# A second tile transposed by TensorE, and loads moved between three DMA queues, in a conditional-mix and paged-attention kernel

## The chip, the cores and the metric

The kernel runs on one core of one Trainium2 chip. A core has five engines that run side by side and wait for one another through semaphores: TensorE (PE; its weight loads are listed as PEld), VectorE (DVE), ScalarE (ACT), GpSimd (POOL) and SyncE (SP), which here only issues DMAs. The metric is the device time of one execution in microseconds (us); the median of several runs counts. The profile is one further execution, with every instruction and every DMA packet recorded.

## The reference

The input `x` has 64 sequences of 32 tokens with 512 channels, in float32. Two layers are added to it in turn:

```python
# layer 0: a matrix chosen per sequence mixes its 32 rows
x = x + einsum('bct,bcd->bdt', x, weights[condition])
# layer 1: attention over a paged cache
q = rope(rmsnorm(x @ Wq.T))            # 32 heads of 128
k = rope(rmsnorm(x @ Wk.T)); v = x @ Wv.T   # 8 heads of 128
kc, vc = k_cache[block_table], v_cache[block_table]   # 16 pages of 32 keys per sequence
scores = q . [kc, k] / sqrt(128)       # 4 query heads share a key head
scores = where(valid, scores, -1e30)   # cached keys: position < cache_seqlens
x = x + (softmax(scores) @ [vc, v]) @ Wo.T
```

The sequence lengths run from 207 to 1644 and the cache holds 512 keys for each sequence, so many sequences have some masked keys. Where the sums of the exponentials leave a safe range, the kernel runs a second, exact pass; with these inputs it is not entered, and its code is only counted by a test at the end.

## The kernel before, in words

Four sequences (32 rows each) make a tile of 128 rows, so there are 16 tiles (`NT`). The eight key heads are done in two halves (`NHH`) of four (`GH`), each with its four query heads (`REP`). A `Step` is one tile in one half: steps 0 to 15 are the first half, steps 16 to 31 the second. In the second half a step doesn't mix and transpose its input again: it reads the transposed tile `x1t` and the running sum `acc` back from DRAM, where the first half stored them (`x1t_d`, line 371, and `acc_d`, line 532).

For a step the work is as follows.

- `x1_a`, `x1_c`, `x1_b` (lines 344 to 371): load `x`, mix it (`pmix`), transpose it (`px1t`) into `x1t`. In the second half `x1_t` (line 350) loads `x1t` instead. `x1t` has one buffer.
- `k_a`, `q_a(g)`, `v_a` (lines 493 to 507): eight matmuls each of 128 x 512 (four chunks, each in two passes), into one of four PSUM buffers called `pp`; then `norm_rope` (line 409): a square on ACT, a power on POOL, and six operations on VectorE.
- The normalized queries and keys must be transposed into columns, `q_cols` for the first three sequences of the tile and `q_last` for the fourth. `q_cols` has one buffer, `q_last` two. There are two ways. For step 0 (`by_tensor`, line 473), `to_columns` (line 483) transposes a group with four TensorE instructions into PSUM (`pt`) and copies it out with two ACT copies. For all later steps `turn_rows` (line 451) transposes 32 x 32 blocks on VectorE, and `spread` (line 463) puts the blocks in place with 16 DMAs of SP, four for each sequence.
- For each sequence (`Batch`, line 540): 16 K pages are loaded by SP (`load_k`, line 280; two buffers); VectorE copies one head at a time into key order (`head_keys`, line 560); `scores` and `values` are matmuls, with the exponential on ACT between them. The V rows are gathered by POOL with indirect DMAs, 128 rows at a time into one of three buffers called `raw` (`fetch`, line 311), and ACT multiplies them by the mask on the way to their place (`fill`, line 552). `new_scores` and `new_values` do the same for the tile's own 32 keys.
- `out_proj` (line 512): 32 matmuls of 128 x 512 and an add into `acc`.

The order is written out by hand. SP and PE take their instructions in program order throughout; the other engines do so in the opening (up to `opening.close()`, line 864), and afterwards a planner orders them. The opening holds step 0's projections and the first sequences, and also the second step's keys and values (`k_a(second)`, `v_a(second)`, lines 849 to 851).

The loop at line 909 takes a step in 16 slots, four for each sequence (`bt`), one head (`g`) per slot. In each slot stand the scores of this head, one piece of the *next* step from the table `pieces` (line 866), and the values of the head before. So the next step's keys and queries are projected in slots 3 to 7, spread in slots 9 and 11, and its values projected in slot 13. Half of the previous step's output projection stands in slot 8 and half in slot 9. At the start of each `bt` the K pages of the sequence two ahead are issued (`after = Batch(...)`, line 917), so in slot 12 the sixteen pages come before the `x1_t` of slot 13 (line 956) in SP's queue. Step 0 enters the loop at slot 4 and has no output projection in slots 8 and 9.

Weights: `load_w` (line 234) loads a matrix of 1 MB. An output matrix is loaded in parts, each part two DMAs of 256 KB (line 249). In the opening SP loads the query weights of groups 0, 2 and 3 and the values' weights, POOL the keys' weights and query group 1 (lines 765 to 785). The output weights of the second half are loaded by POOL's queue in steps 16 and 17 (`second_outputs`, line 908); they take the place of the first half's, which are used last in slot 9 of step 16, and are themselves used first in slots 8 and 9 of step 17. The page numbers and lengths, from which the rows to gather and the masks are made, are loaded by POOL (`pages_at`, `lens_at`, lines 793 to 796) and used by VectorE in `cached_rows` (line 160).

## Time and profile before

| | us |
|---|---|
| median of 3 runs | 2183.66 (2181.93 to 2184.26) |
| the profiled execution's own time | 2188.01 |
| its span, first to last instruction | 2186.2 |
| granted TensorE clock, mean | 0.995 |
| share of the chain that ended last: PE | 95% |
| the same: DMA / issue / DVE | 2% / 1% / 1% |
| mean of one matmul of 128 x 512 in `pp_q` | 0.594 |
| mean of one transpose `pt` (128 x 128) | 0.272 |
| mean of one VectorE transpose of `rows` | 0.706 |
| mean of one ACT copy of `pt`, 384 / 128 columns | 0.480 / 0.289 |
| DMA moved | 358.78 MB, mean 164 GB/s |

In the page each row names a line of the kernel, an engine, an operation and the tiles as out<-in. "Idle before" is the time for which the engine stood still ahead of that row's instructions, followed by what ended most of it. In a list of waits the columns are the total in us, the number of times, and the longest. In a timeline a row has its start and its length in us, and in brackets the idle time ahead of it. Matmuls overlap in the pipeline, so a group of eight that "takes" 1.06 us lets the next one start after 0.89. A wait for several semaphores is put down to the one that was signalled last, which need not be the one that mattered.

### The profile page before, as it was taken

Reading aid. Unit: us, or ns where it says so; the run is one execution under the profiler, and the core shown is the slowest. Engines: PE = TensorE matmul, PEld = TensorE weight load, DVE = VectorE, ACT = ScalarE, POOL = GpSimd, SP = SyncE. Lnnn points to the kernel's source line nnn. Section 1 sums busy time; section 2 is a strip of 40 time slices with the busy share of each in tenths; the row PEclk is TensorE's granted clock in tenths of the full one; section 3 lists DMA queues with packets and bytes.
Section 4 is the critical chain, followed back from the end, with each engine's and each line's share of the span. In section 5 each row is a group of like instructions: output and inputs, shape, how many; then the busy total and the mean of one; then the engine's idle time right before and its main releaser. Section 6 shows DMA issues by size and latency. Waiting matters only on the chain.

```text
span 2186.2 us, 41553 instructions
## 1 busy us (share of the span) xinstructions
PE 2150.5 (98%) x12970; PEld 1498.3 (69%) x12970; DVE 1199.1 (55%) x2881; ACT 866.9 (40%) x1574; POOL 813.1 (37%) x1024
## 2 busy tenths in 40 slices
PE   8889999999999999999999999999999999999998
PEld 5657776677766677766776667777667777667775
DVE  5655556665465554555554556545556445556442
ACT  3434444444333444333433334443334433334441
POOL 4433333343333433343334434333334333334330
PEclk9999999999999999999999999999999999999999
DMA  8665555556555555556767655555555555555651
GB/s 245 172 166 161 169 159 150 153 159 171 157 152 142 167 161 165 158 146 195 237 176 198 174 154 165 167 163 163 149 158 162 170 163 160 149 160 158 175 159 57
DMA packets 386839, 358.78 MB, mean 164 GB/s; under 512 B 54736, under 2 KB 316896, under 8 KB 386608
## 3 DMA queue, kind: packets, MB, share of 16 engines
q1 hardware_dynamic: 340608, 210.90, 34.3%
q0 software_dynamic: 42992, 140.86, 22.6%
q10 hardware_dynamic: 3008, 4.25, 0.5%
q8 instruction: 106, 1.74, 0.3%
q14 instruction: 125, 1.02, 0.2%
HBM read 302.59 MB, written 12.58 MB: 144 GB/s over the span
## 4 chain that ended last, share of the span: by engine, by line
PE 95%; DMA 2%; issue 1%; DVE 1%; ACT 0%; SPq 0%; POOL 0%; ACTq 0%; DVEq 0%; POOLq 0%
PE po_x L631 21%; PE ps_x L573 20%; PE pout_x L519 20%; PE pp_q_x L404 19%; PE pp_k_x L404 5%; PE pp_v_x L404 5%; PE pnv_x L615 2%; PE psn_x L591 1%; DMA raw_x<-in_vc_dram,v_row 1%; PE pmix_x L360 1%; DMA pages_at<-in_pages_v_dram 0%; DMA x1t_x<-x1t_d 0%; DMA k_t_x<-in_kt_dram 0%; PE px1t_x L368 0%; SPq L468 0%
## 5 line engine op out<-in xcount | busy, mean ns | idle before, releaser
L318 POOL DMA_INDIRECT raw_x<-in_vc_dram,v_row x512 | 538.2, 1051 | 828.3 <-ACT v_x L331 756.2
L581 ACT ACTIVATE pr_x<-ps_x 128x512 f32<-128x512 f32 x512 | 305.7, 597 | 818.2 <-PE ps_x L573 757.3
L631 PEld LDWEIGHTS po_x<-v_x,pr_x 128*128 128x128 f32 x4096 | 516.1, 192 | 129.8 <-issue 115.4
L631 PE MATMUL po_x<-v_x,pr_x 128*128 128x129 f32 x4096 | 551.6, 278 | 4.9 <-ACT v_x L331 1.9
L404 PE MATMUL pp_q_x<-wq_x,x1t_x 128*128 128x512 f32 x1024 | 462.5, 594 | 3.4 <-ACT kh_x L564 3.4
L519 PE MATMUL pout_x<-wo_x,ot_x 128*128 128x512 f32 x1024 | 450.2, 592 | 0.0
L573 PE MATMUL ps_x<-q_cols_x,kh_x 128*128 128x128 f32 x3072 | 405.7, 275 | 0.5 <-ACT q_cols_x L488 0.2
L573 PEld LDWEIGHTS ps_x<-q_cols_x,kh_x 128*128 128x128 f32 x3072 | 376.3, 192 | 17.1 <-issue 16.6
L331 ACT ACTIVATE v_x<-raw_x,valid 128x512 f32<-128x512 f32 x512 | 363.2, 716 | 16.5 <-DMA raw_x<-in_vc_dram,v_row 16.5
L519 PEld LDWEIGHTS pout_x<-wo_x,ot_x 128*128 128x128 f32 x1024 | 189.7, 190 | 214.3 <-issue 214.3
L404 PEld LDWEIGHTS pp_q_x<-wq_x,x1t_x 128*128 128x128 f32 x1024 | 185.4, 191 | 188.8 <-issue 185.2
L566 DVE COPY kh_x<-k_t_x 128x512 f32<-128x512 f32 x506 | 206.1, 417 | 191.8 <-PE ps_x L573 162.0
L649 DVE TENSOR_TENSOR nv_x<-po_x,nv_x 128x258 f32<-128x258 f32 x256 | 108.3, 423 | 317.7 <-PE po_x L631 282.5
L421 POOL TENSOR_TENSOR rs_q_x<-ms_q_x,minus_half 128x4 f32<-128x4 f32 x128 | 140.2, 1096 | 175.9 <-DVE ms_q_x L419 174.8
L414 ACT ACTIVATE sq_q_x<-pp_q_x 128x512 f32<-128x512 f32 x128 | 76.4, 597 | 271.9 <-PE pp_q_x L404 165.3
L573 PE MATMUL ps_x<-q_last_x,kh_x 128*128 128x128 f32 x1024 | 135.2, 275 | 2.9 <-DVE kh_x L566 2.9
L527 DVE TENSOR_TENSOR acc_x<-pout_x,acc_x 128x512 f32<-128x512 f32 x32 | 22.1, 692 | 199.5 <-PE pout_x L519 199.5
L573 PEld LDWEIGHTS ps_x<-q_last_x,kh_x 128*128 128x128 f32 x1024 | 124.6, 192 | 3.1 <-issue 3.1
L404 PE MATMUL pp_k_x<-wk_x,x1t_x 128*128 128x512 f32 x256 | 118.1, 605 | 2.8 <-DMA x1t_x<-x1t_d 2.5
L418 DVE TENSOR_REDUCE ms_q_x<-sq_q_x 128x4 f32<-128x512 f32 x128 | 86.4, 675 | 53.2 <-ACT sq_q_x L414 51.2
L404 PE MATMUL pp_v_x<-wv_x,x1t_x 128*128 128x512 f32 x256 | 115.2, 592 | 0.0
L652 DVE TENSOR_TENSOR o_x<-nv_x,rden 128x256 f32<-128x256 f32 x256 | 108.5, 424 | 6.5
(106 smaller groups left out, 1472.3 us busy)
## 6 DMA issues: line engine op xcount, KB each, us to landing
k_t_x<-in_kt_dram SPq DMA_DIRECT2D x2048, 64.0 KB
q_cols_x<-rows_x SPq DMA_DIRECT2D x372, 80.0 KB
q_last_x<-rows_x SPq DMA_DIRECT2D x124, 80.0 KB
raw_x<-in_vc_dram,v_row POOLq DMA_INDIRECT x512
acc_x<-in_x_dram SPq DMA_DIRECT2D x16, 256.0 KB
x1t_d<-x1t_x ACTq DMA_DIRECT2D x16, 256.0 KB
wo_x<-in_wo_dram SPq DMA_DIRECT2D x16, 256.0 KB
acc_d<-acc_x SPq DMA_DIRECT2D x16, 256.0 KB
```

The lines of the kernel that those rows point to most:

```text
L318: nc.gpsimd.indirect_dma_start(out=raw.rearrange("p g d -> p (g d)"), out_offset=None, in_=vc, in_offset=bass.IndirectOffsetOnAxis(ap=v_ro ...
L331: nc.scalar.activation(v_bufs[b % 2][:, c, :, 0:D], raw, AF.Copy, scale=ok)
L404: nc.tensor.matmul(pp, st.x1t[:, c, :], w[:, c, :], start=(c == 0), stop=(c == KC - 1))
L418: nc.vector.tensor_reduce(ms, sq, AX.X, ALU.add)
L421: nc.gpsimd.tensor_tensor(rs, ms, minus_half, ALU.pow)
L519: nc.tensor.matmul(st.po, st.ot[:, i, :], wt["o", st.hh, i // 4][:, i % 4, :], start=(i == 0), stop=(i == QH - 1),)
L566: last["dve"] = nc.vector.tensor_copy(k, ba.k_raw[:, :, g, :]).ins
L573: nc.tensor.matmul(ps[:, c, :], ba.k[g][:, c * P : (c + 1) * P], queries(ba, g), start=True, stop=True,)
L581: last["act"] = nc.scalar.activation(pr, ps, AF.Exp, scale=SCALE).ins
L631: nc.tensor.matmul(ba.po[:, g % 2, :], ba.pr[g][:, c, :], ba.v_t[:, c, g, :], start=(c == 0), stop=(c == VC - 1),)
L649: nc.vector.tensor_tensor(t, ba.po, t, ALU.add)
L652: nc.vector.tensor_tensor(ba.o[:, both, :], t[:, :, 0:D], rd.unsqueeze(2).to_broadcast([P, 2, D]), ALU.mult,)
```

## The change

Four edits are made together.

1. The second step's keys and queries are transposed as the first step's are: `by_tensor` holds for `st.n < 2`. `pieces(second)` has no `spread`; instead `to_columns` stands in slots 12 (keys, group 0), 13 (group 1) and 14 (groups 2 and 3). The keys are copied out of PSUM by ACT, the four query groups by VectorE. `v_a(second)` moves from the opening to slot 13.
2. In the opening the query weights of group 2 are loaded on POOL's queue, ahead of `pages_at`, instead of SP's.
3. When the sequence two ahead is loaded at the start of slot 12 (`bt == BT - 1`), only its first eight K pages are issued there; the other eight follow in slot 13, behind `x1_t`.
4. The second half's output weights are issued by SP instead of POOL, at other slots: one part in slot 10 of step 16 and seven parts in slots 2 to 7 of step 17.

```diff
--- before.py
+++ after.py
@@ -246,15 +246,15 @@
             if kind == "o" and not exact:
                 src = src.rearrange("(h j p) e -> h p j e", h=REP, p=S)
                 for h in range(part.start, part.stop):
-                    eng.dma_start(t[h * S : (h + 1) * S, :, :], src[h])
+                    nc.sync.dma_start(t[h * S : (h + 1) * S, :, :], src[h])
                 return
             eng.dma_start(t[:, part, :], src.rearrange("(c p) e -> p c e", p=P)[:, part, :])
 
-        def load_parts(which, hh, at, eng=nc.sync):
+        def load_parts(which, hh, at):
 
             if 0 <= at < 2 * len(which):
                 kind, g = which[at // 2]
-                load_w(kind, hh, g, slice(at % 2 * 2, at % 2 * 2 + 2), eng)
+                load_w(kind, hh, g, slice(at % 2 * 2, at % 2 * 2 + 2))
 
         outputs = [("o", g) for g in range(GH)]
 
@@ -277,7 +277,7 @@
 
         last_k = []
 
-        def load_k(hh, b):
+        def load_k(hh, b, first_pages):
             k_raw = kv.tile([P, NPP, GH, PSIZE], F32, tag="k_t", name=f"k_t_{hh}_{b}_{uid}")
 
             with ExitStack() as order:
@@ -290,7 +290,7 @@
                     max_val=PAGES - 1,
                     skip_runtime_bounds_check_because="a block table names pages of the cache",
                 )
-            for j in range(NPP):
+            def load_page(j):
                 ins = nc.sync.dma_start(
                     k_raw[:, j, :, :].rearrange("p g r -> p (g r)"),
                     kt[hh, bass.ds(page[j], 1)].rearrange("o d e -> (o d) e"),
@@ -303,8 +303,11 @@
                             bass.ds(page[j], 1), hh
                         ].rearrange("o r g d -> (o r) g d"),
                     )
-            last_k[:] = [ins.ins]
-            return k_raw
+                last_k[:] = [ins.ins]
+
+            for j in range(first_pages):
+                load_page(j)
+            return k_raw, [lambda j=j: load_page(j) for j in range(first_pages, NPP)]
 
         raws = {}
 
@@ -471,7 +474,7 @@
                     )
 
         def by_tensor(st):
-            return st.n == 0 or exact
+            return st.n < 2 or exact
 
         def finish(st, i, pp, name, kind):
 
@@ -480,15 +483,13 @@
             else:
                 turn_rows(st, i, norm_rope(st, pp, name, kind), name)
 
-        def to_columns(st, i):
+        def to_columns(st, i, copy=nc.scalar.copy):
 
             pt = transposed(rows[:, :, i, :], f"{i}_{st.name}")
             p4 = pt.rearrange("p h (b s) -> p b h s", b=BT)
             n = BT - 1
-            nc.scalar.copy(q_cols[:, :, i, :].rearrange("p b (h s) -> p b h s", h=4), p4[:, 0:n])
-            nc.scalar.copy(
-                columns(st, n)[:, i, :].rearrange("p (h s) -> p h s", h=4), p4[:, n]
-            )
+            copy(q_cols[:, :, i, :].rearrange("p b (h s) -> p b h s", h=4), p4[:, 0:n])
+            copy(columns(st, n)[:, i, :].rearrange("p (h s) -> p h s", h=4), p4[:, n])
 
         def k_a(st):
             name = f"k_{st.name}"
@@ -540,12 +541,12 @@
         class Batch:
 
 
-            def __init__(self, st, bt):
+            def __init__(self, st, bt, first_pages=NPP):
                 self.st, self.bt = st, bt
                 self.n = st.n * BT + bt
                 self.name = f"{st.name}_{bt}"
                 self.b = st.t * BT + bt
-                self.k_raw = load_k(st.hh, self.b)
+                self.k_raw, self.pages_left = load_k(st.hh, self.b, first_pages)
                 self.k, self.pr = {}, {}
                 self.v_t = v_bufs[self.b % 2]
 
@@ -777,8 +778,8 @@
         nc.scalar.dma_start(cond_row, cond.rearrange("(i s) t -> s t i", s=S)[0:1])
         load_w("k", 0, eng=nc.gpsimd)
         load_w("q", 0, 1, eng=nc.gpsimd)
+        load_w("q", 0, 2, eng=nc.gpsimd)
         batch = Batch(first, 0)
-        load_w("q", 0, 2)
         load_w("v", 0)
         x1_a(second)
         load_w("q", 0, 3)
@@ -848,7 +849,6 @@
         rot_tables(second)
         k_a(second)
         q_b(first, 3)
-        v_a(second)
         scores(batch, 3)
         new_scores(first)
         scores(later, 0)
@@ -864,7 +864,21 @@
         opening.close()
 
         def pieces(st):
-            do = {
+            if st is second:
+                by_vector = nc.vector.tensor_copy
+                return {
+                    4: (lambda st: q_a(st, 0),),
+                    5: (lambda st: q_a(st, 1),),
+                    6: (lambda st: q_a(st, 2),),
+                    7: (lambda st: q_a(st, 3),),
+                    12: (lambda st: to_columns(st, GH), lambda st: to_columns(st, 0, by_vector)),
+                    13: (v_a, lambda st: to_columns(st, 1, by_vector)),
+                    14: (
+                        lambda st: to_columns(st, 2, by_vector),
+                        lambda st: to_columns(st, 3, by_vector),
+                    ),
+                }
+            return {
                 2: (rot_tables,),
                 3: (k_a,),
                 4: ((q_a, 0),),
@@ -875,9 +889,6 @@
                 11: ((spread, (2,)),),
                 13: (v_a,),
             }
-            if st is second:
-                do[2] = do[3] = do[13] = ()
-            return do
 
         def count(hh):
 
@@ -905,7 +916,14 @@
         load_cond_weights(2)
         for at in (3, 4, 5):
             load_parts(outputs, 0, at)
-        second_outputs = [(0, 10), (0, 13), (0, 15), (1, 1), (1, 3), (1, 4), (1, 5), (1, 6)]
+        second_outputs = {
+            (0, 10): (0,),
+            (1, 2): (1,),
+            (1, 4): (2,),
+            (1, 5): (3, 4),
+            (1, 6): (5, 6),
+            (1, 7): (7,),
+        }
         for st in steps:
             ahead = steps[st.n + 1] if st.n + 1 < len(steps) else None
             beyond = steps[st.n + 2] if st.n + 2 < len(steps) else None
@@ -914,7 +932,7 @@
                 this, after = batch, None
                 n = st.n * BT + bt + 2
                 if n < NHH * NT * BT:
-                    after = Batch(steps[n // BT], n % BT)
+                    after = Batch(steps[n // BT], n % BT, NPP // 2 if bt == BT - 1 else NPP)
                     unfilled += [(after, c) for c in range(VC)]
                 for g in range(GH):
                     slot = bt * GH + g
@@ -952,8 +970,11 @@
                             load_cond_weights(beyond.t)
                         if slot == 11:
                             x1_a(beyond)
-                    if slot == 13 and beyond:
-                        x1_t(beyond)
+                    if slot == 13:
+                        if beyond:
+                            x1_t(beyond)
+                        for load in after.pages_left if after else ():
+                            load()
                     if slot == 14 and beyond:
                         x1_c(beyond)
                     if slot == 15 and beyond:
@@ -962,9 +983,8 @@
                         count(0)
                     if st.n == 1 and slot in (4, 5):
                         load_parts(outputs, 0, slot + 2)
-                    if (st.n - NT, slot) in second_outputs:
-                        at = second_outputs.index((st.n - NT, slot))
-                        load_parts(outputs, 1, at, nc.gpsimd)
+                    for at in second_outputs.get((st.n - NT, slot), ()):
+                        load_parts(outputs, 1, at)
                     if st.n in (NT - 2, NT - 1):
                         load_parts(
                             [("k", 0), ("q", 0), ("q", 1), ("q", 2), ("q", 3), ("v", 0)],
```

## The prediction

> **What bounds the kernel now.** I read the page first, then the waits of TensorE (longest first), a table of busy time by stretch, the TensorE and SP timelines around the holes, and the chain of waits.
>
> ```profile
> span 2186.2 us, 41553 instructions
> PE 2150.5 (98%) x12970; PEld 1498.3 (69%) x12970; DVE 1199.1 (55%) x2881; ACT 866.9 (40%) x1574; POOL 813.1 (37%) x1024
> ...
> PE psn_x L591 <- DMA q_cols_x<-rows_x: 7.7, 1, 7.7
> PE pp_q_x L404 <- ACT kh_x L564: 3.4, 1, 3.4
> PE ps_x L573 <- DVE kh_x L566: 2.9, 1, 2.9
> PE pp_k_x L404 <- DMA x1t_x<-x1t_d: 2.5, 1, 2.5
> ...
> 64.73:85.58 20.85, 20.26 (x91) 12.42 (x90) 10.11 (x23) 7.75 (x14) 8.39 (x9) 1.00 0.83 200
> 85.58:107.59 22.01, 16.32 (x137) 15.33 (x135) 16.82 (x43) 10.20 (x18) 11.48 (x15) 1.00 0.60 166
> 107.59:120.21 12.62, 4.88 (x51) 4.05 (x50) 0.79 (x3) 2.48 (x5) 1.89 (x2) 0.73 0.59 162
> 184.40:187.39 2.99, 2.99 (x51) 2.67 (x49) 0.00 (x0) 2.42 (x4) 1.37 (x2) 1.00 0.84 258
> ...
> 7.01 8.96 DMA pages_at<-in_pages_v_dram
> 107.62 2.58 DMA x1t_d<-x1t_x
> 1193.25 7.60 DMA x1t_x<-x1t_d
> ...
> 39.83 0.60 PE L448 MATMUL pt_x<-ident,rows_x 128*128 128x128 f32 x4
> 40.27 1.02 PE L360 MATMUL pmix_x<-acc_x,bd 128*128 128x512 f32 x2
> 1200.99 5.37 PE L404 MATMUL pp_k_x<-wk_x,x1t_x 128*128 128x512 f32 x8 [2.45 <-DMA x1t_x<-x1t_d]
> ```
>
> TensorE is busy 2150.5 of 2186.2 us; only its 36 us of holes can be won. Four lie at the places that the diff touches. The table (length, then busy time of PE, PEld, DVE, ACT, POOL) covers the slots of the first tile: slots 4 to 7, 8 to 15, and from the scores of slot 0 of the second tile to those of slot 1. That last stretch took 12.62 us; the third tile does the same 51 matmuls in 2.99 us. So the second tile's new scores cost 9.6 us: a wait of 7.7, the rest matmuls at a reduced clock.
>
> **The skill.** "TensorE: Matmul & The Clock Gate", Part 1, says that an idle window of about 3.4 us halves the clock and that the window runs freely. The trace agrees, phase included: after the 2.45 us hole at 1201 eight pp_k matmuls end 5.2 us later, where 3.5 is usual, while the 2.9 us hole at 97.5 cost nothing more. Its Part 4 gives some 275 ns for a TensorE transpose; pt_x has 272 ns. "DMA: Bandwidth & Descriptors", Queues, rings and completion order: each ring is served in order, and an engine takes turns between the rings. The trace agrees: pages_at, issued behind two weights on GpSimd's queue, lands 8.96 us later.
>
> **The change part by part.**
>
> *Third query weights (1 MB) from SP to GpSimd's queue, ahead of pages_at.* The 3.4 us hole at 29.86 is put down to an ACT copy ending at 29.77, but that instruction also waits for the weights, which SP issued at 22.48 and which land at 29.72. In the new place they land near 18.6: wk and wq1 landed 3.1 us apart on that queue, so one more megabyte costs 3.1. The same 3.1 us falls on pages_at, which lands at 19.1 instead of 15.97. Behind it in order on VectorE stand v_row, the masks, the second angles and, through ACT's sine, the first norm; its rows, done at 25.17, move to 28.2, and the transposes in front of the third projection to 28.3. That projection then starts at about 29.0 instead of 29.86: 0.9 us gained. GpSimd's four gathers move from 16.7 to 19.8 and are over before its power is due. SP's 16 K page loads share the engines and end some 3 us later, but VectorE and ACT want them at 32. Ends: 3.4 gained if pages_at is not held up, 1.5 lost if the megabyte takes 5.5 us.
>
> *v_a(second) leaves the opening.* Its eight matmuls, 3.44 us (52.98 to 56.41), go. The scores behind it then wait 0.8 for ACT's copies of the last columns (end 53.87), so slot 4 starts 2.7 earlier. The gathers at 65.74 to 68.38, which shared the engines with six wo loads of SP issued at 64.5 (the first took 8.3 us), now go out at about 62, ahead of them, so the 0.6 us wait for v_x in slots 4 to 7 goes as well. Slot 8 starts at 85.58 - 0.9 - 2.7 - 0.6 = 81.4.
>
> *Slots 8 to 15.* Holes before: 22.01 - 16.32 = 5.7 us. ACT stood behind a late gather until 74.0, so VectorE began its norms at 75.3 and then ran almost without a pause to 97. Five 32x32 transposes of 0.71 us each leave it, and it starts some 6 us earlier; the holes from it should go. The gathers remain: three buffers, 4 to 6 us from issue to landing, one per slot of 1.8 us. I leave 2.5 us of holes (ends 0 and 5.7). Added work: four transposes take 0.44 us (39.83 to 40.27), so 20 take 2.2; v_a comes back with 3.44. Evacuation: ACT needs 0.47 + 0.28 for one group; four groups on VectorE I put at 0.55 + 0.3 each, between the 258-element add from PSUM (423 ns) and the 512-element ones (680 ns): 3.4 us in three slots that now last 11, beside matmuls. Four PSUM buffers go round among nine users; a late copy would cost up to 2 us, counted in the ends. Slot 16 starts at 107.59 - 4.2 - 3.2 + 5.6 = 105.8.
>
> *New scores of the second tile.* The 16 DMAs of spread go. SP's records show why they were late: each DMA of SP or ACT first waits for the one that last used its semaphore, of eight taken in turn, and the ninth spread DMA waited for the x1t_d store (107.62, landing 2.58 later). Columns that come through PSUM have no such queue, so 9.6 us go. SP gets 10 us of issue time back; the K pages that began at 116.45 start earlier, and what is late next (VectorE waits 1.4 us for pages at 127) is covered too. Slot 1 starts at 105.8 + 2.99 = 108.8 instead of 120.21: **11.4 us gained**.
>
> *x1t between halves of the pages.* At 1193.25 x1t_d was issued behind 16 page loads begun at 1181.67. With eight ahead of it, it goes out near 1187 (v_a, which frees its buffer, ends at 1183.9), and even with 7.6 us lands at 1194.6; TensorE wants it at 1198.5. Gain 2.45 + 1.7 for the clock = **4.15 us**. The other eight pages lose one issue of 0.4 us; their copies are due at 1200. In the other steps of the second half v_a is over before the eighth page is issued, so SP waits for nothing new.
>
> *Second output weights by SP.* 16 DMAs at 0.6 us leave POOL (not a bound) and cost SP 0.47 each. Twelve fall between 1216, where SP had issued the second batch's pages, and 1225.2, until which it waited for a VectorE copy: 5.6 us in a hole of 9. As all 12 need 8 semaphores, the pages behind wait for landings; at the 1.45 us per 256 KB load seen at 70 to 77 us they drain at 1217 + 17.4 = 1234, and the last pages and 12 spread DMAs end near 1247, where the last four wait for slot 11 anyway. Cost 0; ends 0 and 10 (a late spread, with its clock).
>
> Sum: -11.4 - 4.15 = -15.5 us. The profiled execution took 2188.01 (span 2186.2 and 1.8 around it), 4.35 above the median of 2183.66; the holes are taken to be the same in both. 2183.66 - 15.5 = **2168**.
>
> **Rivals.** (a) The likeliest, above: 2168, own range 2163 to 2172. (b) Slots 8 to 15 stay bound by gathers and copies: all 5.7 us of holes stay, a PSUM wait of 2 comes on top, the opening gives nothing: -15.5 + 3.2 + 2 + 0.9 = -9.4, 2174. For it: three gather buffers, and gathers that end holes on the chain; against it: the wo loads and spreads that slowed them are moved or gone. (c) SP falls behind at the second weights by one late spread: -15.5 + 10 = -5.5, 2178. (d) Slower: the same queue, with 256 KB taking more than twice 1.45 us because gathers and pages share the engines. SP then leaves its 12 loads at 1252 instead of 1234, and pages, spread and x1t all come some 18 us late in that tile; it decides from the point where the delay at slot 11 passes 16 us, plus the clock: 2186 and up. Against it: the engines moved 300 to 400 GB/s when full at 10 to 14 us. (e) The opening gains its full 3.4 and no hole is left in 8 to 15: -20.5, 2163.
>
> **How the numbers follow.** (a) 0.60, (b) 0.17, (e) 0.08, (c) 0.08, (d) 0.07. The predicted time is that of (a). Range 2162 to 2177: it takes in (a), (b) and (e); (c) and (d) lie outside. About 0.2%, 4.4 us, is what a measurement can tell from no change; (c) is split over same and faster. Faster 0.88, same 0.05, slower 0.07.
>
> **What would show it.** Right: no wait of psn_x for a DMA, slot 1 of the second tile near 109 us; pages_at landing near 19; pp_k near 1197 with no wait for x1t_x; 20 more pt_x. Wrong: holes before po_x or ps_x between 81 and 106 above 5 us; a hole at psn_x near 1255 or at pout_x after 1228; VectorE's copies of pt_x above 0.7 us with TensorE waiting for them.

## The result, and the profile after

| | before | after |
|---|---|---|
| median (us) | 2183.22 (2181.93 to 2184.26, 4 runs) | 2167.95 (2166.54 to 2169.00, 4 runs) |
| the profiled execution's own time | 2188.01 | 2166.54 |

The ratio is 0.993, with a 95% interval of 0.9915 to 0.9945: 15.3 us less between the medians, where 15.5 had been forecast. (The prediction had three runs of the kernel before, with a median of 2183.66; a fourth brought it to 2183.22.) The profiled executions are 21.5 us apart. That difference between 15.3 and 21.5 is part of what has to be explained.

The head of the page after (the second line gives each engine's busy time, share of the span and instructions), then the longest waits of TensorE (total, times, longest):

```profile
span 2164.8 us, 41582 instructions
...
PE 2145.4 (99%) x12990; PEld 1497.4 (69%) x12990; DVE 1196.6 (55%) x2884; ACT 863.0 (40%) x1576; POOL 805.5 (37%) x1009
```

```profile
PE pmix_x L363 <- DVE bd L803: 3.2, 1, 3.2
PE pt_x L451 <- DVE rows_x L443: 2.5, 1, 2.5
PE ps_x L574 <- ACT q_cols_x L491: 1.6, 3, 0.8
```

TensorE's holes shrink from 35.7 us (2186.2 - 2150.5) to 19.4 (2164.8 - 2145.4). Its busy time falls by 5.1 us although 20 transposes were added. Matmuls that no longer run at the reduced clock are 3.7 us of that at two places (the second tile's new scores, 4.88 busy before and 2.99 now, and the `pp_k` behind `x1t`, 5.37 and 3.60). The waits for `psn_x` and `x1t_x` are gone from the list. The `pt_x` wait of 2.5 us is new.

The stretches that the prediction used, at their new places (length, then busy time of PE, PEld, DVE, ACT, POOL, the granted clock, DMA share and GB/s). The last row lies around the second output weights:

```profile
61.60:81.59 19.99, 19.99 (x91) 12.35 (x90) 13.08 (x33) 8.45 (x15) 10.61 (x11) 1.00 0.87 221
81.59:102.89 21.30, 21.30 (x165) 18.84 (x163) 14.73 (x39) 10.76 (x20) 9.38 (x13) 1.00 0.67 189
102.89:105.88 2.99, 2.99 (x50) 2.67 (x49) 0.00 (x0) 2.31 (x5) 1.37 (x2) 1.00 0.34 108
...
1196.00:1240.00 44.00, 44.00 (x240) 30.43 (x242) 24.15 (x57) 14.50 (x24) 14.59 (x19) 1.00 0.85 203
```

In all four rows the length equals the PE column: TensorE has no hole there. In the whole trace it has none above 0.06 us after 59.1 us. Slots 8 to 15 hold 5 us more work than before (21.30 against 16.32 busy) in 0.7 us less time. The stretch with the second tile's new scores, 12.62 us before, takes 2.99. Side by side, with what the prediction said:

| place | before | after | moved by | predicted |
|---|---|---|---|---|
| scores of slot 4 | 64.73 | 61.60 | -3.1 | -3.6 |
| scores of slot 8 | 85.58 | 81.59 | -4.0 | -4.2 |
| scores of slot 16 | 107.59 | 102.89 | -4.7 | -1.8 |
| scores of slot 1, second tile | 120.21 | 105.88 | -14.3 | -11.4 |
| gained more between there and the `x1t` load of step 17 | | | -1.0 | 0 |
| gained at that load | | | -4.4 | -4.15 |
| the rest of the span, to its end | | | -1.8 | 0 |

The last row is the difference of two things: TensorE's own work gains 2.6 us more, 1.57 of it a hole at 2133 us that only the first profile has, and what follows TensorE's last matmul takes 0.8 us longer (9.5 us against 8.7).

The opening, from the chain of waits (start, length) and from TensorE's timeline (start, length, then the hole in front in brackets), with the first use of the loaded `x1t`:

```profile
7.71 11.25 DMA pages_at<-in_pages_v_dram
```

```profile
28.33 0.86 PE L451 MATMUL pt_x<-ident,rows_x 128*128 128x128 f32 x4 [2.53 <-DVE rows_x L443]
28.98 5.10 PE L407 MATMUL pp_q_x<-wq_x,x1t_x 128*128 128x512 f32 x8
...
1183.09 3.60 PE L407 MATMUL pp_k_x<-wk_x,x1t_x 128*128 128x512 f32 x8
```

`pages_at` lands at 18.96 and the third projection starts at 28.98, both within 0.2 us of the forecast. But the projection's eight matmuls take 5.10 us and not 3.60: the hole of 2.53 us in front of them has cost the clock. The `pp_k` matmuls at 1183.09 follow the work before them with no hole.

SP's queue around the second output weights (start, time from the first to the last of a run of DMAs, what they load, how many):

```profile
1198.08 8.80 SPq L249 DMA_DIRECT2D wo_x<-in_wo_dram  x12
1208.93 14.15 SPq L294 DMA_DIRECT2D k_t_x<-in_kt_dram  x16
1223.20 5.71 SPq L471 DMA_DIRECT2D q_cols_x<-rows_x  x8
...
1232.19 2.94 SPq L471 DMA_DIRECT2D q_cols_x<-rows_x  x4
```

The twelve loads take 8.80 us of SP's time, and the sixteen pages behind them 14.15 us, where the sixteen ahead of them took 9.85. Before, the spread of that tile began at 1233.52, which is 1213.8 once the 19.7 us by which the whole program is earlier are taken off. So it now starts some 9.4 us late, and the last four DMAs of it some 4.6 us late. TensorE does not notice (the last row of the table by stretch): these columns are needed only by the next tile, and no hole stands there either.

### The profile page after: what moved, and what is told of

Its sections match the earlier page's. It is cut to its first block, busy times and chain, and to the rows that moved or that the text cites. A ratio compares the mean times of both kernels' runs of the same rounds, so it can differ in the third digit from the quotient of the medians.

```text
span 2164.8 us, 41582 instructions
## 1 busy us (share of the span) xinstructions
PE 2145.4 (99%) x12990; PEld 1497.4 (69%) x12990; DVE 1196.6 (55%) x2884; ACT 863.0 (40%) x1576; POOL 805.5 (37%) x1009
## 4 chain that ended last, share of the span: by engine, by line
PE 97%; DVE 1%; DMA 1%; ACT 0%; issue 0%; POOL 0%; DVEq 0%; ACTq 0%
PE po_x L632 22%; PE ps_x L574 21%; PE pout_x L520 20%; PE pp_q_x L407 20%; PE pp_v_x L407 5%; PE pp_k_x L407 5%; PE pnv_x L616 2%; PE psn_x L592 1%; PE pmix_x L363 1%; DMA pages_at<-in_pages_v_dram 1%; PE px1t_x L371 0%; DMA cond<-in_cond_dram 0%; PE pt_x L451 0%; ACT sq_q_x L417 0%; ACT q_cols_x L491 0%
## 5 line engine op out<-in xcount | busy, mean ns | idle before, releaser
L653 DVE TENSOR_TENSOR o_x<-nv_x,rden 128x256 f32<-128x256 f32 x256 | 108.8, 425 | 6.2
```

The lines of the kernel that those rows point to most:

```text
L653: nc.vector.tensor_tensor(ba.o[:, both, :], t[:, :, 0:D], rd.unsqueeze(2).to_broadcast([P, 2, D]), ALU.mult,)
```

## The experiments

Each kernel ran five rounds beside the kernel before. In the three groups of runs the kernel before had medians of 2184.02, 2184.18 and 2183.87 us. "Position" below is where a kernel stands against the first profile of before, by the start of the same matmuls.

### The first edit alone, and the third alone

The first edit in the kernel before:

```diff
-            return st.n == 0 or exact
+            return st.n < 2 or exact
...
-        v_a(second)
...
+                    12: (lambda st: to_columns(st, GH), lambda st: to_columns(st, 0, by_vector)),
+                    13: (v_a, lambda st: to_columns(st, 1, by_vector)),
```

> The kernel before with edit 1 alone: second tile by TensorE, its value projection moved to slot 13. Theory A (the parts add up): 10 to 14 us faster than before, 2169 to 2173; no wait of psn_x for a DMA; the hole of some 3.4 us before the third query projection stays, and the wait for x1t_x near 1190 us may stay. Rival B (the gain in front needs the earlier query weights as well, because the freed time falls into that hole): less than 8 us faster. Rival C (the gain of the whole change comes mostly from the second half, the profiled execution of before being an odd one in front): less than 5 us faster.

2168.99 us (2165.89 to 2172.72), ratio 0.9935 (0.9917 to 0.9953): 15.0 us from one edit of four. Its position is -15.5 once the second tile has begun, so the whole front gain is the first edit's; there is no wait for `psn_x` and no hole between slots 8 and 16. Behind the opening one hole remains, and it is longer than before's (timeline of TensorE, then of SP, in this kernel):

```profile
1187.58 5.34 PE L404 MATMUL pp_k_x<-wk_x,x1t_x 128*128 128x512 f32 x8 [5.16 <-DMA x1t_x<-x1t_d]
```

```profile
1165.33 11.82 SPq L294 DMA_DIRECT2D k_t_x<-in_kt_dram  x16
1177.26 0.37 SPq L354 DMA_DIRECT2D x1t_x<-x1t_d  x1
```

`x1t` is issued behind sixteen pages whose issue took 11.82 us, and TensorE has it only 10.3 us later: it stands 5.16 us and then works at the reduced clock. In the changed kernel the load goes out at 1170.22, behind eight pages, 12.9 us ahead of its first use.

The third edit in the kernel before:

```diff
-                    after = Batch(steps[n // BT], n % BT)
+                    after = Batch(steps[n // BT], n % BT, NPP // 2 if bt == BT - 1 else NPP)
...
-                    if slot == 13 and beyond:
-                        x1_t(beyond)
+                    if slot == 13:
+                        if beyond:
+                            x1_t(beyond)
+                        for load in after.pages_left if after else ():
+                            load()
```

> The kernel before with edit 3 alone: eight of the sixteen K pages behind the load of x1t. Theory A: the wait of pp_k_x for x1t_x goes in step 17 and with it the matmuls at half clock, 3 to 5 us faster, 2178 to 2180. Rival D (that wait belongs to the one execution that was profiled, or comes from the wo loads on the other queue and not from the place of x1t behind the pages): within 1.5 us of before.

2180.59 us (2173.51 to 2183.82), ratio 0.9982 (0.9968 to 0.9996): 3.4 us less, within an interval of 0.9 to 7.0. The wait for `x1t` is gone from the trace. The waits for `psn_x` are all there (8.8 us in two). This trace shows them well, in SP's queue and then in SP's waits between 95 and 110 us:

```profile
93.84 6.11 SPq L471 DMA_DIRECT2D q_cols_x<-rows_x  x8
104.25 2.41 SPq L471 DMA_DIRECT2D q_last_x<-rows_x  x4
```

```profile
SPq L471 <- DMA x1t_d<-x1t_x: 4.3, 1, 4.3
```

Eight DMAs of the spread go out by 99.95. Then SP stands for 4.3 us until ACT's store of `x1t_d` lands, and the ninth goes out at 104.25. The last four are issued by 109.2 and `psn` resumes at 110.76.

### What held the spread

The prediction said that the ninth DMA waited for its semaphore, last used by ACT's store of `x1t_d`. So only that store, for the third tile, was put on GpSimd's queue in the kernel before:

This is what the profile of before shows of it, in SP's queue and in SP's waits between 95 and 117 us:

```profile
97.23 6.51 SPq L468 DMA_DIRECT2D q_cols_x<-rows_x  x8
110.22 2.41 SPq L468 DMA_DIRECT2D q_last_x<-rows_x  x4
```

```profile
SPq L468 <- DMA x1t_d<-x1t_x: 6.5, 1, 6.5
```

The DMAs of SP and ACT name eight semaphores in turn. By these names the store comes between the first and the second DMA of the spread, and the ninth is the next one that needs the store's semaphore; but ACT issued the store only at 107.62. The edit:

```diff
-            nc.scalar.dma_start(x1t_d[st.t], ...
+            by = nc.gpsimd if st.n == 2 and not exact else nc.scalar
+            by.dma_start(x1t_d[st.t], ...
```

> The kernel before, in which the store of the third tile's x1t to DRAM is issued by GpSimd instead of ACT; nothing else. Theory A (SP's spread DMAs of the second tile stood behind that store, whose semaphore came next in turn): the wait of psn_x for q_cols_x falls from 7.7 us to below 3, 5 to 9 us faster than before, 2174 to 2178. Rival E (the spread is late because its rows or the slot-11 scores are late): the wait stays at 6 to 8 us and the time within 1.5 us of before.

2180.32 us (2177.99 to 2185.43), ratio 0.999 (0.9982 to 0.9997). The wait became 5.1 us, from 7.7: neither theory's number. SP's queue in this kernel, and the hole in TensorE's timeline:

```profile
96.29 5.17 SPq L469 DMA_DIRECT2D q_cols_x<-rows_x  x8
102.02 2.42 SPq L469 DMA_DIRECT2D q_last_x<-rows_x  x4
104.54 3.24 SPq L469 DMA_DIRECT2D q_cols_x<-rows_x  x4
```

```profile
112.39 0.42 PE L592 MATMUL psn_x<-q_cols_x 128*32 128x128 f32 x1 [5.12 <-DMA q_cols_x<-rows_x]
```

The pause between the eighth and ninth DMA, 6.5 us before (103.74 to 110.22), is 0.6 us, so the store was what held it: the prediction's mechanism is shown. But it was only the last bound of two. With it gone the sixteen DMAs still start right behind sixteen pages (ended at 96.1), take 11.5 us to issue and 4.6 more until TensorE runs. Only taking the columns off SP's queue removes both, as the first edit does.

### The second edit

It was tried from both sides: alone in the kernel before, and undone in the changed kernel, with the changed kernel itself run again beside it.

```diff
         load_w("k", 0, eng=nc.gpsimd)
         load_w("q", 0, 1, eng=nc.gpsimd)
+        load_w("q", 0, 2, eng=nc.gpsimd)
         batch = Batch(first, 0)
-        load_w("q", 0, 2)
```

Alone:

> The kernel before with edit 2 alone: third query weights on GpSimd's queue ahead of pages_at. Theory A: pages_at lands at 18.5 to 19.5 us instead of 16, the transposes ahead of the third projection start near 28.3, and the projection near 29 instead of 29.9: 0.5 to 1.5 us earlier there; in the total 0 to 1.5 us faster, 2182 to 2183. Rival F (the weights alone held that projection): the projection starts near 26.5, 3 us or more faster. Rival G (pages_at late costs more behind it than the weights gain): 1 us or more slower.

Undone in the changed kernel (the same diff, reversed):

> The changed kernel with edit 2 undone: third query weights on SP's queue behind the K pages. Prediction's step: 0.9 us slower than the changed kernel. Rival H (pages_at, which edit 2 delays by 3 us, costs what the weights gain; edit 1 alone reached the second tile's new scores at 102.8 us, the changed kernel at 103.9): 0 to 2 us faster than the changed kernel.

The changed kernel again:

> The changed kernel once more, beside the ones that undo a part of it. Theory A: 14 to 17 us faster than before in the medians; its trace has no hole at psn_x and none at pp_k_x near 1183 us, as in the first one. Rival C (the first profile was a lucky one): holes at one of these places again, or less than 12 us faster.

| kernel | median | ratio | third projection starts |
|---|---|---|---|
| before + second edit | 2184.78 (2178.35 to 2190.72) | 1.0001 (0.9989 to 1.0014) | 29.14 |
| changed kernel | 2167.25 (2166.59 to 2168.76) | 0.9922 (0.9907 to 0.9937) | 29.06 |
| changed, second edit undone | 2165.78 (2165.26 to 2167.72) | 0.9915 (0.9900 to 0.9930) | 29.13 |

The edit is worth nothing that these runs can tell. TensorE's timeline at the third projection, first with the edit alone, then in the changed kernel without it:

```profile
28.67 0.63 PE L448 MATMUL pt_x<-ident,rows_x 128*128 128x128 f32 x4 [4.39 <-DVE rows_x L440]
29.14 5.29 PE L404 MATMUL pp_q_x<-wq_x,x1t_x 128*128 128x512 f32 x8
```

```profile
24.95 0.63 PE L451 MATMUL pt_x<-ident,rows_x 128*128 128x128 f32 x4 [0.68 <-DVE rows_x L443]
29.13 5.37 PE L407 MATMUL pp_q_x<-wq_x,x1t_x 128*128 128x512 f32 x8 [3.55 <-DMA wq_x<-in_wq_dram]
```

The hole is of a similar size (4.39 and 3.55 us; 2.53 and 4.09 in two traces of the changed kernel); it only moves. Without the edit the transposes stand at 25 and the projection waits for its weights. With it the weights are early, but `pages_at` and with it the first tile's norms come 3.4 us later (ACT's first square is at 23.91 in the first trace of the changed kernel and at 20.54 without the edit). Over all traces the projection starts at 28.65 to 29.60 with this edit (five traces, middle one 29.06) and at 28.27 to 30.56 without (seven, 29.13).

Two kernels asked whether the weights can have both. In the first the third query weights follow `pages_at` and `lens_at` on GpSimd's queue in the changed kernel; the second also moves the four loads of the next mixing matrix behind the second sine on ACT:

```diff
-        load_w("q", 0, 2, eng=nc.gpsimd)
...
         nc.gpsimd.dma_start(lens_at, lens_row.partition_broadcast(P))
+        load_w("q", 0, 2, eng=nc.gpsimd)
```

> The changed kernel with the third query weights on GpSimd's queue behind pages_at and lens_at instead of ahead of them. Theory A (in the changed kernel pages_at and the norm chain behind it hold the third projection): pages_at lands near 16, the weights near 20, the third projection starts near 26.3 without a hole and at full clock, and slot 8 is reached 3 to 4.5 us earlier, 2164 or 3 to 4.5 us faster than the changed kernel. Rival J (the norms on VectorE bind right behind it, so that the gain is lost by 42 us, or the gathers now behind 1 MB are late): within 1 us of the changed kernel.

```diff
-        load_cond_weights(1, nc.scalar, mybir.EngineType.Activation)
...
         angles(TRIG, trig)
+        load_cond_weights(1, nc.scalar, mybir.EngineType.Activation)
```

> The changed kernel with the third query weights behind the page numbers and lengths on GpSimd's queue, and with the four loads of the second tile's mixing matrix issued by ACT after the second sine instead of ahead of it. Theory A, that the sine (and with it the chain of norms of the first tile) waited for those DMAs from 18.98 to 22.25: the sine now starts near 20.4, right behind its angles, rows_x of the first group ends near 25.5, the first transposes stand at 25.7 to 26.2, without a hole or with one under 0.5, provided the weights have landed; the third projection then starts at 26.2 to 28. Then the first new scores of the tile come 1.0 to 1.8 earlier than in the version with the weights moved alone, and the total is 2164 to 2166. Rival B: the third query weights land only near 28 in this place, so the hole moves to pp_q and nothing is gained: 2166 to 2168. Rival C: something behind it in the opening (ACT's copies, the mixing matrix itself for pmix near 37) holds TensorE instead, and the gain is handed back by 54 us.

The first gave 2166.77 us (2165.52 to 2168.05), ratio 0.9919 (0.9904 to 0.9934). The hole in front of the transposes falls to 1.7 us and the projection, at 27.97, runs at the full clock (3.60 us), but a wait of 1.8 us for ACT's copies at 40.12 takes most of it back: the first new scores come 0.8 us earlier (53.5 against 54.3). That is the rival's side. The second gave 2171.63 us (2170.42 to 2172.13), ratio 0.9941 (0.9928 to 0.9954), some 4 us worse than the changed kernel (0.9922). ACT's timeline in the two kernels (the second group is the second kernel):

```profile
18.98 3.21 ACTq L271 DMA_DIRECT2D bd<-in_w_cond_dram  x4
22.24 0.31 ACT L150 ACTIVATE sin<-trig 128x128 f32<-128x128 f32 x1 [7.07 <-DMA bd<-in_w_cond_dram]
...
23.09 0.58 ACT L417 ACTIVATE sq_q_x<-pp_q_x 128x512 f32<-128x512 f32 x1
```

```profile
20.57 0.31 ACT L150 ACTIVATE sin<-trig 128x128 f32<-128x128 f32 x1 [5.74 <-DMA x1t_d<-x1t_x]
...
23.11 3.25 ACTq L271 DMA_DIRECT2D bd<-in_w_cond_dram  x4
26.41 0.60 ACT L417 ACTIVATE sq_q_x<-pp_q_x 128x512 f32<-128x512 f32 x1 [4.90 <-DMA bd<-in_w_cond_dram]
```

The sine did start at 20.57, as theory A had it. But the four DMAs keep ACT for 3.2 us at either place, and now the first square stands behind them: at 26.41 instead of 23.09. The Trainium skill, "TensorE: Matmul & The Clock Gate", Part 1, Architectural detail, says that ScalarE takes its instructions strictly first in, first out; the trace agrees. Moving a blocking issue past one waiter had put it in front of the next, which was due sooner. The kernel with the loads moved to a place where ACT has nothing due was not tried.

### The fourth edit

The changed kernel with the second output weights back on GpSimd's queue and at their old slots:

```diff
-                    for at in second_outputs.get((st.n - NT, slot), ()):
-                        load_parts(outputs, 1, at)
+                    if (st.n - NT, slot) in second_outputs:
+                        at = second_outputs.index((st.n - NT, slot))
+                        load_parts(outputs, 1, at, nc.gpsimd)
```

> The changed kernel with edit 4 undone: the second half's output weights by GpSimd's queue at the old slots. Prediction's step: edit 4 is worth nothing, within 1 us of the changed kernel, and no wait for x1t_x, since edit 3 alone removes it. Rival I (the wo loads of the old slots are what makes x1t late and the engines full at 1175 to 1186 us): a hole of 2 us or more at pp_k_x or po_x between 1170 and 1240, 2 to 6 us slower than the changed kernel.

2167.68 us (2164.80 to 2171.68), ratio 0.9924 (0.9907 to 0.9941), against 2167.25 with the edit: no difference in the median. Its trace has a wait of 1.4 us for VectorE's `kh` at 1189.6 that the changed kernel's has not, at the end of a stretch (1170 to 1190) in which the DMA engines are full: a share of 1.07, where the changed kernel has 0.75. The next kernel, with the same placement, shows a wait of 1.1 there. The runs lie further apart (6.9 us against 2.2). Whether the edit steadies the kernel can't be settled by six runs each.

### The first and third edits together

The kernel before with the hunks of these two edits, none of the others:

```diff
-            return st.n == 0 or exact
+            return st.n < 2 or exact
...
-                    after = Batch(steps[n // BT], n % BT)
+                    after = Batch(steps[n // BT], n % BT, NPP // 2 if bt == BT - 1 else NPP)
```

> The kernel before with edits 1 and 3 alone (the third query weights stay on SP's queue, the second half's output weights stay on GpSimd's). Theory A, from the single edits: edits 2 and 4 are worth nothing, so this is the changed kernel's time, 2165 to 2169, ratio 0.9915 to 0.993, and the two wins add: 15.0 for edit 1 and 3.4 for edit 3 would give 2165.8. No wait for x1t near 1181, the first new scores of the second tile near 103.5, with no DMA wait. Rival: edits 2 and 4 together bring what each alone doesn't show; then it stays above 2170, at edit 1 alone (2169) or worse.

2167.77 us (2166.72 to 2168.36), ratio 0.9924 (0.9911 to 0.9936): the changed kernel's time, with two of its four edits. No wait for `psn_x`, none for `x1t_x`. The two single gains, 15.0 and 3.4, would add to 18.4; together they give 16.1, and the intervals allow either.

### The values' projection kept in the opening

The changed kernel, with `v_a(second)` where it was:

```diff
         q_b(first, 3)
+        v_a(second)
...
-                    13: (v_a, lambda st: to_columns(st, 1, by_vector)),
+                    13: (lambda st: to_columns(st, 1, by_vector),),
```

> The changed kernel with the second tile's values projected in the opening again, as before, and not in slot 13; everything else as changed. Theory A: moving the eight matmuls is neutral, since TensorE has no hole left in slots 8 to 15 that they could fill and the opening is bound by TensorE as well: slot 4 starts 2.5 to 3.4 later (64 to 65), slot 16 within 1 of 102.9, total within 2 of the changed kernel (2165 to 2169). Rival B: the v_a matmuls of slot 13 cover TensorE's waits for the columns; without them there are waits for q_cols or kh of 1 to 4 us in slots 12 to 16 and the total is 1 to 4 longer. Rival C, the prediction's reading that v_a leaves holes in the opening: the gathers that are issued later bring back the 0.6 us wait for v_x in slots 4 to 7 and 1 to 2.5 us of holes in slots 8 to 15.

2167.25 us (2165.95 to 2169.87), ratio 0.9922 (0.9909 to 0.9936): in the medians nothing, as theory A said. Its trace, though, looks like rivals B and C. Without the eight matmuls in slot 13, two holes stand in slots 8 to 15:

```profile
93.26 1.13 PE L574 MATMUL ps_x<-q_last_x,kh_x 128*128 128x128 f32 x8 [1.43 <-DVE kh_x L567]
99.23 0.49 PE L632 MATMUL po_x<-v_x,pr_x 128*128 128x129 f32 x2 [1.08 <-ACT v_x L334]
```

They are 2.5 us together, and the second tile begins 2.4 us later than in the changed kernel (of which 0.6 was there at the third projection already). Of the eight traces with `v_a` in slot 13, seven have no hole in slots 8 to 15, and the eighth, in which the sine was moved, has one of 1.7 us. So the move of `v_a` seems to fill holes that would otherwise be there, though only this one trace has it in the opening together with the first edit. That it is worth 2 us in one trace and nothing in the medians stays unexplained.

### A second profile of the kernel before

The kernel before as it is, with no edit:

> The kernel before once more, for a second profile of it. Theory A, that the profiled execution of before was an unlucky one: its 1.6 us hole near 2133 (values behind the exponential) is absent here, and the 0.4 us one near 1066 may be; the holes at the four edited places are present with sizes that vary by a few us; the profiled time is 2 to 6 below 2188.0. Rival: the same holes with the same sizes and a profiled time within 1 of 2188; then the profile's surplus over the median comes from profiling itself. Ratio 1.000 within 0.002 in either case.

Its profiled execution took 2177.99 us, 10.0 less than the first one, while its median (14 runs) is 2183.33 (2177.99 to 2191.35), ratio 1.000 (0.9989 to 1.0012). Its waits:

```profile
PE psn_x L591 <- DMA q_cols_x<-rows_x: 8.2, 2, 6.6
...
PE pp_k_x L404 <- DMA x1t_x<-x1t_d: 2.4, 1, 2.4
```

The holes for `psn_x` and for `x1t_x` are there again. But there is no hole at 2133 us, where the first profile has one of 1.57 in front of `po_x`; the eight matmuls behind the `x1t` wait took 3.67 us, not 5.37; and of the 5.7 us of holes in slots 8 to 15 only 0.5 us is left. Against this execution the changed kernel's profile gains 9.6 us at the front, 2.6 more at `x1t`, and 11.4 over the span (0.8 is lost behind TensorE's last matmul), where it had gained 21.4 against the other. The median's 15.3 lies between. Theory A holds, by more than it expected.

## Why the prediction was right, and where it was not

- **Where the gain comes from: right.** Nearly all is the first edit (15.0 us alone), through the wait of `psn_x`, and the third removes the wait for `x1t`; the two together give the whole (16.1). Single traces agree. The second tile's output projection starts at 147.8 to 152.9 us in the five traces without the first edit and at 137.1 to 143.5 in the nine with it, and the wait for `x1t` of step 17 stands in all five traces without the third edit (2.4 to 5.2 us) and in none of the nine with it. Both mechanisms, the queue of SP and the semaphore last used by the store, were seen in the experiments; of the semaphore the prediction missed that a second bound, the issue and landing of the spread itself, lies 2.6 us behind it.
- **Slots 8 to 15: too careful.** "I leave 2.5 us of holes (ends 0 and 5.7)" was the term that was mis-sized: none was left, and slot 16 came at 102.89 instead of 105.8. The kernel with `v_a` in the opening has those 2.5 us of holes; with `v_a` in slot 13 TensorE has other work at that time. And the 5.7 us that the term starts from were the most that any trace shows: over the five without the first edit these holes add up to 0.1 to 5.7 us, so part of what was gained there is not the change's. That same term is why slot 1 came at 105.88 instead of 108.8.
- **Third query weights: the place right, the gain not there.** All the times of that step were met (18.96, 28.3, 28.98). But 0.9 us was read off one execution of before; over seven traces without the edit the third projection starts between 28.27 and 30.56. And the new hole brings the clock down as the old one did, which the prediction's own paragraph on the clock would have allowed it to say.
- **`v_a` out of the opening:** slot 4 was forecast 3.6 us earlier with the weights' share and came 3.1 earlier; slot 8 4.2 and 4.0.
- **Copies by VectorE:** put at 0.55 and 0.3 us; 0.558 and 0.282 in the trace, and no wait of TensorE is put down to one of them; for ACT's copies it waits at most 0.8 us at a time. **Transposes:** twenty, with a median of 0.273 us, as taken.
- **`x1t`:** 4.15 forecast, 4.4 in the profile. Against the second profile of before it is 2.6, and in the medians 3.4 with a wide interval: the hole, and the 1.7 us for the clock most of all, vary from one execution to the next.
- **Second output weights: cost 0 was right,** though the drain was not. SP did not have to drain to 1234 at 1.45 us per load: it issued twelve in 8.8 us, and the delay fell on the pages behind (14.15 us). Rivals (c) and (d) needed a spread so late that TensorE waits; it was 9.4 us late at its start and 4.6 at its end, and nobody waited.
- **"The holes are taken to be the same in both"** (the profiled execution and the median) was wrong. The profile that the sum was made against was one of the longer executions of before, with holes that had nothing to do with the change and others that were larger than usual. Against it the change brought 21.5, 6 us more than forecast; against the median 15.3. The forecast of 2168 was met because two errors offset each other: holes of before that were larger than in the mean, and an estimate of what would remain that was larger than what did. That it came within 0.3 us is luck.

Not settled are the values of the second and fourth edits (the second alone lies between 2.4 us faster and 3.1 us slower; the fourth was only undone, and the intervals with and without it overlap), and by how much the third helps in the mean.

## What to carry to other kernels

Before a sum is made of the holes in a trace, ask which of them another execution would have: those behind a chain of DMAs came out at 2.4 to 5.2 us for the same wait (`x1t`), and the clock behind them cost nothing or 1.6 to 1.8. Where columns go by small DMAs on a queue that also carries the pages, taking them through PSUM pays more than freeing the one DMA that waited last, since the next bound stood 2.6 us behind. And before a load or a blocking issue is moved, look at what is next in order on that engine: the loads that were taken from in front of the sine stood in front of the square.

## What was not expected of the hardware

**A hole of 2.4 to 3.0 us may or may not cost the clock.** The Trainium skill ("TensorE: Matmul & The Clock Gate", Part 1, What's actually happening) gives a freely running window of about 3.4 us, and the reduced clock after an idle one. In these traces the eight projection matmuls behind a hole, some with four transposes between, are a probe (only those of which all eight are recorded; the last column is explained below):

| hole in front (us) | the eight matmuls | busy share of the emptiest window |
|---|---|---|
| 0.61, 1.72, 2.00 | full clock, 3.60 to 3.67 us | 0.63 to 0.82 |
| 2.40, 2.92, 2.98 | full clock, 3.67 us | 0.45 to 0.57 |
| 2.45, 2.53, 2.68 | reduced, 5.37, 5.10 and 4.79 us | 0.26 to 0.28 |
| ten of 3.08 to 5.20 | reduced, 5.16 to 5.37 us | 0 to 0.33 |

All holes over 3 us were paid for with 1.6 to 1.8 us more, and none up to 2.0. Between them it was one or the other, at nearly the same length (2.40 and 2.45).

What decides can be read from the same traces, since they record when the granted clock changed. In all fourteen the changes lie whole multiples of 3.41 us apart, which is the freely running window. Cut on that grid, a hole counts by how much it takes out of one window: the last column has the share of the window for which TensorE was busy. Here are one window with the hole and the one behind it, for the hole of 2.45 us in before, then for that of 2.98 us in the kernel with the moved store (length and PE busy come first; the clock is the number behind the last bracket):

```profile
1198.33:1201.74 3.41, 0.96 (x4) 0.50 (x4) 1.55 (x4) 1.43 (x4) 1.71 (x2) 1.00 1.14 282
1201.74:1205.16 3.42, 3.42 (x5) 1.33 (x4) 0.00 (x0) 0.00 (x0) 0.04 (x1) 0.50 1.04 228
```

```profile
1194.63:1198.04 3.41, 1.52 (x4) 0.83 (x5) 0.72 (x2) 0.00 (x0) 1.49 (x2) 1.00 1.12 210
1198.04:1201.46 3.42, 3.42 (x16) 1.99 (x15) 0.60 (x1) 0.88 (x2) 0.00 (x0) 1.00 1.09 191
```

The shorter hole lay whole in one window and left TensorE 0.96 us of work in it; the clock was halved over the next. The longer one was shared by two windows, and the emptier of them still had 1.52 us of work. In the table a window that was busy for up to 0.33 of its length is followed by the reduced clock, and one that was busy for 0.45 or more is not. The skill speaks of an idle window; by these runs it need not be idle throughout. The prediction's two examples (2.45 and 2.9 us, shares of 0.28 and 0.52) fit. This is not the whole rule where small matmuls (`psn`, `pnv`) stand in a window: in seven of the fourteen traces the clock is also reduced behind one that ends between 57 and 65 us, was busy for 0.72 or 0.73 and holds those of `pnv`. What such matmuls count for was not separated.

**SP's pages stood still behind GpSimd's weights.** The prediction took it that the engines take turns between the rings. The DMA view of before between 10 and 12 us shows something else for that stretch (queue: packets, MB, share of sixteen engines; then what was issued in that time):

```profile
q0 software_dynamic: 215, 0.82, 102.7%
...
k_t_x<-in_kt_dram SPq DMA_DIRECT2D x5, 64.0 KB
```

It is the only queue listed: for two microseconds only GpSimd's queue moved packets, at 0.41 MB per us, though SP issued five pages in that time and three in the two microseconds ahead. From 12.2 us on their packets run beside those of the weights: between 12 and 14 us GpSimd's queue moved 174 packets with 0.68 MB, SP's 139 with 0.07. The counts are of a like size, as turns packet by packet would have it, but the pages' packets are much smaller, so the weights keep most of the bandwidth. Why none ran before 12.2 us is not shown. For the prediction's own steps it did not matter, since they rest on the order within GpSimd's queue.
